# A window-attention and Fourier kernel: from row 19 on, transfers issued in the program's order

## Chip, cores and metric

The kernel runs on one core of a Trainium2 chip. The metric is the device time of one execution in microseconds, the median over runs. Everything is float32.

## What is computed

The input x is 32 images of 56 x 56 positions with 128 channels. Two layers are applied one after the other, each on a group-normalised copy of x (groups of 4 channels) and each added back to x.

```python
# layer 0: shifted 7x7-window attention, 4 heads of 32 channels, with position bias and shift mask
x = x + attention(_gn(x), rpb_table, w_qkv, w_proj, b_proj)

# layer 1
def _forward_fourier(x, w0, w1):          # x is (B, I, M, N) here
    x_fty = dct(x, norm='ortho', axis=-1)
    out_y = einsum('bixy,ioy->boxy', x_fty[..., :32], w0)
    xy = idct(out_y padded to N, norm='ortho', axis=-1)
    ...                                    # the same along the other axis with w1: xx
    return xx + xy

def _feedforward(x, W1, b1, W2, b2):       # 128 -> 512 -> 128
    return relu(x @ W1 + b1) @ W2 + b2

x = x + _feedforward(_forward_fourier(_gn(x), w0, w1), W1, b1, W2, b2)
```

## The kernel before

An image is cut into 8 rows of windows (7 lines of 56 positions each). The program is one software pipeline over *cycles*. In cycle n, row n of all images in sequence (row n mod 8 of image n div 8) gets its q, k and v, its scores and its maximum; row n-1 its exponentials; row n-2 its transpose; row n-3 its product with v, its projection and the residual sum (`attn_project`); row n-4 its sums and squares for the second normalisation. The second layer of an image starts 11 cycles after the first row of the image (`CONV_BEGIN`) and takes 16 cycles, so that two images are in it at a time; c counts its cycles. The DCT along the width is done at c = 0, along the height at c = 1 and 2, the mixing of modes at c = 3, 4 and 5, the way back at c = 5, 6, 7, 10 and 12, and the feed-forward product in seven groups of tokens at c = 8, 9, 10, 12, 13, 14 and 15. In this text *row k* stands for a cycle whose number is k modulo 8, so that c = 0 falls into rows 3, c = 1 into rows 4, c = 5 into rows 0.

Up to cycle 18 a head of its own (`first_rows`, `next_rows`) fills the pipeline. The loop from cycle `HEAD_END` = 19 on is the steady state: `halves_first`, `eighths`, `quarters`, `behind_max` and `halves_last` write down one cycle's work. When no rows are left for projection, the loop takes a branch of its own that ends each cycle with `load_first`, `last_out` and `load_back`: the drain.

The order of the instructions on PE, ACT, DVE and POOL is the order in which the program writes them (`manual_schedule`). SP, which issues nearly all transfers, is in program order only until cycle 10; then `in_order.close()` leaves its order to a scheduler, which moves transfers past each other by its own estimate of when each can run. Whatever the order, SP is one queue: an issue that waits for a semaphore holds all that stand behind it. Each transfer also carries one of eight completion semaphores in turn, and waits for the transfer eight places before it.

The transfers of the steady state are:

- `xin`, a quarter of the next image: `load_quarter` (L160) issues four transfers of 112 KB, with runs of 128 bytes, into a single buffer; `turn_quarter` transposes it on DVE (L424 to L429) into the window layout `xw`. Which quarter is turned in which row is a table, `next_steps`: in row 0 the first (0, 0) early in the row and the second (0, 1), called *late*, behind the maximum; in row 4 the third, in row 5 the fourth. A quarter that is turned early is loaded by `next_begin` at the end of the row before; a late one by `next_quarter` in its own row.
- `xr`, tokens of x for the residual sum of the row that is projected next cycle: `load_tokens` (L137), called by `next_tokens`; POOL adds the projection's bias (L143). The buffer's last reader is `sum_squares` on DVE (L752).
- `scr<-x`, the first layer's result (L722), stored to DRAM behind each projection.
- `htok`, the same result read back as columns for the DCT along the height (`load_columns`, L859, 2 x 392 KB): the first half in row 3, the second in row 4 once PE has used the first (L825), for one buffer.
- `zscr<-z` and `zT<-zscr`: mixed modes stored (L882) and read back (`load_modes`, L893, by `load_back`) for the way back on PE (`modes_back`, L911), with two buffers.
- `res`, the tokens to which the feed-forward result is added (`ff_in`, L944 and L949), two buffers; POOL adds a bias (`ff_bias`, L961), DVE adds the product (L1008, L1018), and `ff_out` stores to the output (L1024 to L1039, `out_dram<-res`).

In `ff_in` the load of `res` is written ahead of the matmuls of the same group; a scheduler may issue it earlier, as soon as the buffer is free.

Of the kernel before, what the change touches and what calls it, by code (L numbers as in the profile page):

```python
# [50 lines left out]
def swin_fourier_kernel(  # L51
# [33 lines left out]
    ET = mybir.EngineType  # L85
# [15 lines left out]
    def conv_bank():  # L101
        return conv_banks[next(conv_turns) % 4]
# [47 lines left out]
    def load_quarter(b, k, u):  # L150

        if b > 1:
            t = work.tile([P, HW, KB], F32, tag="xin", name="xin", bufs=1)
        else:
            t = y_of[k][:, : S * KB].rearrange("p (w c) -> p w c", w=S)
            t = t[:, u * HW : (u + 1) * HW]
        rows = slice(k * (S - KB), k * (S - KB) + KB)
        for cb in range(C // KB):
            cs = slice(cb * KB, (cb + 1) * KB)
            nc.sync.dma_start(t[cs], x[b, rows, u * HW : (u + 1) * HW, cs])  # L160
        return t
# [34 lines left out]
    xins = {}  # L196
# [741 lines left out]
    def ff_in(im, g):  # L938
        t0, n = sum(FF_GROUPS[:g]), FF_GROUPS[g]
        k, last = n // P, n % P  # L940
        xff = im.xf.rearrange("p r w -> p (r w)")
        scr_tok = im.scr.rearrange("h w c -> (h w) c")
        res = work.tile([P, 4, C], F32, tag="res", name="res")
        nc.sync.dma_start(  # L944
            res[:, :k], scr_tok[t0 : t0 + k * P].rearrange("(n p) c -> p n c", p=P)
        )
        if last:
            for hs in HALVES:
                nc.sync.dma_start(res[hs, k, :JP], scr_tok[t0 + k * P : t0 + n, hs])  # L949
        im.res = res  # L950
        im.hid = []
        for f in range(NF):
            ph = conv_bank()
            halved(ph[:, :n], wff1[:, f * P : (f + 1) * P], xff[:, t0 : t0 + n])
            hf = work.tile([P, HB], F32, tag="hid", name="hid", bufs=NF)
            nc.scalar.activation(hf[:, :n], ph[:, :n], AF.Relu, bias=b1sb[:, f : f + 1])  # L956
            im.hid.append(hf)
# [123 lines left out]
    def next_tokens(cycle):  # L1081
        im, i = row(cycle - 2)
        if im:
            load_tokens(im, i)
# [6 lines left out]
    def halves_first(cycle):  # L1091
        begins = [im for im, c in fourier(cycle) if c == 0]
        last, j = row(cycle - 4)
        if cycle % NWR == NWR - 1:
            norm_step(cycle)
        tokens_bias(cycle)
        im, i = row(cycle)
        behind_short = im and i == NWR - 1
        if behind_short:
            attn_q(im, i)  # L1100
            attn_exp(cycle - 1)
        if (cycle - 1) % NWR not in EARLY:
            divide(cycle)
        if last:
            attn_sums(last, j)
        next_quarter(cycle)
        if im:
            if not behind_short:
                attn_q(im, i)
            attn_k(im, i)  # L1110
            if i == NWR - 2:
                wrap_rows(cycle)
        late = squares_late(cycle)
        if last and not late:
            attn_squares(last, j)
            sum_squares(last, j)
        if not late:
            next_tokens(cycle)
        if cycle % NWR == 0:
            norm_step(cycle)  # L1120
        for im, c in fourier(cycle):
            if c in FF_AT:
                ff_in(im, FF_AT.index(c))
        for im in begins:
            if cycle > HEAD_END:
                start_stats(im)
# [102 lines left out]
    def next_steps(cycle):  # L1229
        b, i = divmod(cycle, NWR)  # L1230
        steps = {
            0: ((0, 0), (0, 1), ()),
            1: (None, None, (0, 1, 2, 3)),
            4: ((1, 0), None, ()),
            5: ((1, 1), None, (4, 5)),
            6: (None, None, (6, 7)),
        }
        if b == 0:
            steps[0] = (None, None, ())
            steps[1] = ((0, 0), None, ())  # L1240
            steps[2] = ((0, 1), None, ())
            steps[3] = (None, None, (0, 1, 2, 3))
        if b == 1:
            steps[0] = ((0, 0), None, ())
            steps[1] = ((0, 1), None, ())
            steps[2] = (None, None, (0, 1, 2, 3))
        none = (None, None, ())
        return (b + 1, *(steps.get(i, none) if b + 1 < NB else none))

    def next_quarter(cycle):  # L1250
        b, quarter, late, _ = next_steps(cycle)
        if quarter:
            turn_quarter(images[b], *quarter)
        if late and (b, *late) not in xins:
            xins[(b, *late)] = load_quarter(b, *late)

    def wrap_rows(cycle):
        b = next_steps(cycle)[0]
# [63 lines left out]
    HEAD_END = CONV_BEGIN + FF_AT[0]  # L1322
# [79 lines left out]
    def next_rows(cycle):  # L1402
        c = cycle - CONV_BEGIN
        first = images[0]
        im, i = row(cycle)
        im3, i3 = row(cycle - 3)
        last, j = row(cycle - 4)
        attn_q(im, i)
        attn_k(im, i)
        if i == NWR - 2:  # L1410
            wrap_rows(cycle)
        attn_exp(cycle - 1)
        scale_head(first, c, False)
        next_quarter(cycle)
        attn_values(im3, i3, cycle - 3, i in VALUES_BY_ACT)
        tokens_bias(cycle)
        if c == 0:
            for h in range(2):
                transform(first, True, h)
        if c in (1, 2):  # L1420
            transform(first, False, c - 1)
            if c == 1:
                load_columns(first, 1)
        attn_scores(im, i, cycle)
        attn_max(cycle)
        for h in range(2 if c == 0 else 0):
            for r in range(2):
                turn_modes(first, True, h, r)
        for r in range(2):
            columns_turn(cycle, r)  # L1430
        turn(cycle)
        for width, g in back_groups(c):
            modes_back(first, width, g)
            fetch_back(first, width, g)
        if c == 3:
            half_columns(cycle)
        if c:
            attn_squares(last, j)
            attn_sums(last, j)
        divide(cycle)  # L1440
        if c:
            sum_squares(last, j)
            if j < NWR - 1:
                add_sums(last, j)
        next_tokens(cycle)
        next_groups(cycle)
        if i == NWR - 1:
            for _ in range(2):
                norm_step(cycle)
        attn_v(im, i, cycle)  # L1450
        if i == NWR - 1:
            norm_step(cycle)
        if i == 0:
            norm_step(cycle)
        if c == 0:
            start_stats(first)
            next(first.stats)
            next(first.stats)
            load_first(cycle)
        if c != 3:  # L1460
            half_columns(cycle)
        half_columns(cycle, True)
        scale_head(first, c, True)
        load_back(cycle + 1)
        next_begin(cycle)
        attn_project(im3, i3)
        if cycle == HEAD_END - 1:
            attn_exp(cycle)
# [35 lines left out]
    in_order.close()  # L1504
    for cycle in range(CONV_BEGIN, HEAD_END):
        next_rows(cycle)
    for cycle in range(HEAD_END, NB * NWR + CONV_BEGIN + FF_AT[-1] - NWR + 1):
        halves_first(cycle)
        if not row(cycle - 3)[0]:
            eighths(cycle)  # L1510
            for r in range(2):
                columns_turn(cycle, r)
            behind_max(cycle)
            quarters(cycle)
            last_fetch(cycle)
            half_columns(cycle)
            half_columns(cycle, True)
            scale_first(cycle, 0)
            scale_first(cycle, 1)
            load_first(cycle)  # L1520
            last_out(cycle)
            load_back(cycle + 1)
            continue
        if not has_ff(cycle):
            half_columns(cycle)
        eighths(cycle)
        early = any(c == 10 for _, c in fourier(cycle))
        if early:
            columns_turn(cycle, 0)
        quarters(cycle)  # L1530
        if row(cycle)[0]:
            attn_max(cycle)
        if not early:
            columns_turn(cycle, 0)
        columns_turn(cycle, 1)
        last_fetch(cycle)
        if squares_late(cycle):
            sum_squares(*row(cycle - 4))
            next_tokens(cycle)
        behind_max(cycle)  # L1540
        load_first(cycle)
        halves_last(cycle)
# [62 lines left out]
```

## Time and profile before

| what | value |
|---|---|
| time, median of 3 runs | 3221.83 us (3219.25 to 3224.47) |
| the profiled execution | 3222.57 us, span 3220.8 us |
| busy in the span | PE 3162.6, weight loads 2369.0, DVE 2508.5, ACT 2189.3, POOL 2280.0 us |
| PE busy in 0 to 200 us | 158.0 us |
| transfers of the SP queue | 437 MB, 57% of the 16 engines' time |
| packets under 512 bytes | 513,296 of 1,160,384 |
| largest waits of SP | 626.6 us for DVE at L1032; 125.5 us for DVE at L137; 89.0 us for DVE at L160 |
| POOL's wait for `res` (L961) | 77.8 us in 12 waits, 10.7 at the longest |

A busy engine in this table is the union of its instructions' times. The span is that of the program's instructions, and the time around it is 1.8 us. An image takes eight rows, about 97 us of the steady state. The lines of the trace are those of the listing above; `SPq` names an issue by SP, which counts as idle time of SP's engine.

### The profile page before, as it was taken

What the parts mean: (1) busy time and instruction counts of PE and PEld (TensorE: products, weight loads), DVE (VectorE), ACT (ScalarE), POOL (GpSimd) and SP (SyncE); (2) the same over time, 40 slices, a digit from 0 to 9 for tenths busy, and PEclk for the clock granted to TensorE, in tenths of its full rate; (3) what the DMA queues carried; (4) which work ended last, traced back from release to release, by engine and by line L of the source; (5) the groups of instructions that cost most, each with busy time, mean ns of one, the idle gap of its engine ahead of it and who ended that gap; (6) DMA issues with size and microseconds to landing.
All of it is one profiled execution on the core that took longest, in us unless ns stands there. A gap on an engine that the chain in (4) does not pass through costs nothing.

```text
span 3220.8 us, 152669 instructions
## 1 busy us (share of the span) xinstructions
PE 3162.6 (98%) x65968; PEld 2369.0 (74%) x65968; DVE 2508.5 (78%) x4753; ACT 2189.3 (68%) x4018; POOL 2280.0 (71%) x2552
## 2 busy tenths in 40 slices
PE   7899999999999999999999999999999999999999
PEld 5667777777777777777777777777777777777776
DVE  7668888888888788888888888887888888887751
ACT  5566676676777666777766776666777666776664
POOL 5547777777777777777777777777777777777741
PEclk9999999999999999999999999999999999999999
DMA  6555665665666666556656566655556655565453
GB/s 131 111 128 132 146 141 140 141 147 141 144 142 144 138 143 148 141 141 144 140 141 148 140 141 144 140 145 145 138 140 149 139 143 141 142 144 139 123 139 102
DMA packets 1160384, 448.29 MB, mean 139 GB/s; under 512 B 513296, under 2 KB 1129857, under 8 KB 1159709
## 3 DMA queue, kind: packets, MB, share of 16 engines
q1 hardware_dynamic: 1157715, 437.49, 57.0%
q8 instruction: 517, 8.47, 1.2%
q14 instruction: 158, 1.29, 0.1%
q10 hardware_dynamic: 1642, 0.94, 0.1%
q0 software_dynamic: 352, 0.09, 0.0%
HBM read 276.77 MB, written 161.48 MB: 136 GB/s over the span
## 4 chain that ended last, share of the span: by engine, by line
PE 94%; DVE 2%; issue 1%; DMA 1%; POOL 1%; ACT 1%; SPq 0%; DVEq 0%; POOLq 0%; ACTq 0%
PE pc L129 41%; PE pa L129 10%; PE pa L545 8%; PE pc L872 7%; PE pa L567 6%; PE pa L706 6%; PE pa L661 5%; PE pc L911 5%; PE pc L825 3%; PE pc L632 1%; DMA xin<-in_x_dram 1%; PE pc L998 0%; ACT k L532 0%; PE pa L772 0%; PE pc L400 0%
## 5 line engine op out<-in xcount | busy, mean ns | idle before, releaser
L616 POOL TENSOR_TENSOR blocks<-a,rs 32x272 f32<-32x272 f32 (+3 forms) x1416 | 1202.3, 856 | 379.1 <-DVE rs L599 257.1
L129 PE MATMUL pc<-xf,wff 128*64 128x512 f32 (+2 forms) x3584 | 714.3, 539 | 0.0
L129 PE MATMUL pc<-wff,hid 128*64 128x128 f32 x12288 | 712.8, 273 | 1.3 <-issue 0.6
L129 PEld LDWEIGHTS pc<-wff,hid 128*64 128x64 f32 x12288 | 680.2, 137 | 8.2 <-issue 2.9
L586 POOL TENSOR_TENSOR a<-a,mx 128x784 f32<-128x784 f32 x249 | 374.8, 1505 | 303.6 <-DVE mx L585 289.5
L129 PEld LDWEIGHTS pc<-xf,wff 128*64 128x64 f32 x3584 | 264.9, 136 | 368.9 <-issue 293.7
L956 ACT ACTIVATE hid<-pc,b1sb 128x512 f32<-128x512 f32 (+2 forms) x896 | 500.2, 642 | 42.0 <-PE pc L129 41.9
L129 PE MATMUL pa<-xw,wn 128*64 128x392 f32 x2048 | 392.5, 498 | 8.2 <-ACT wn L498 8.1
L575 DVE TENSOR_TENSOR a<-pa,bm 128x392 f32<-128x392 f32 x498 | 257.7, 559 | 170.4 <-PE pa L567 157.8
L552 ACT COPY v<-pa 128x512 f32<-128x512 f32 x256 | 151.6, 592 | 287.4 <-PE pa L545 278.9
L143 POOL TENSOR_TENSOR xr<-xr,bproj 128x384 f32<-128x384 f32 (+1 forms) x256 | 292.5, 1142 | 59.0 <-DMA xr<-in_x_dram 35.3
L532 ACT ACTIVATE k<-pa,bqkv,heads 128x392 f32<-128x392 f32 x512 | 318.5, 673 | 16.2 <-ACT q L519 1.4
L961 POOL TENSOR_TENSOR res<-res,b2sb 128x512 f32<-128x512 f32 (+1 forms) x224 | 251.8, 1124 | 83.4 <-DMA res<-scr 77.8
L847 ACT ACTIVATE y<-modes,rstd 128x448 f32<-128x448 f32 x256 | 276.8, 1141 | 44.8 <-DVE modes L840 31.3
L519 ACT ACTIVATE q<-pa,bqkv 128x392 f32<-128x392 f32 x256 | 149.7, 585 | 231.3 <-PE pa L129 229.2
L592 ACT ACTIVATE a<-a 128x784 f32<-128x784 f32 x249 | 213.2, 856 | 128.0 <-POOL a L586 127.9
L644 DVE STREAM_TRANSPOSE eT<-blocks 128x1024 f32<-128x1024 f32 x237 | 291.2, 1229 | 0.0
L545 PE MATMUL pa<-wn,xw 128*64 128x128 f32 x4096 | 285.4, 280 | 4.2 <-issue 3.1
L661 PEld LDWEIGHTS pa<-eT,v 49*32 49x32 f32 x16384 | 172.6, 105 | 150.8 <-issue 66.8
L597 DVE TENSOR_REDUCE sm<-a 128x16 f32<-128x784 f32 x249 | 238.5, 958 | 45.9 <-ACT a L592 45.3
L545 PEld LDWEIGHTS pa<-wn,xw 128*64 128x64 f32 x4096 | 222.3, 137 | 40.2 <-issue 4.8
L585 DVE TENSOR_REDUCE mx<-a 128x16 f32<-128x784 f32 x249 | 241.1, 968 | 7.6
(136 smaller groups left out, 5017.3 us busy)
## 6 DMA issues: line engine op xcount, KB each, us to landing
zscr<-z SPq DMA_DIRECT2D x512, 112.0 KB
xin<-in_x_dram SPq DMA_DIRECT2D x480, 112.0 KB
htok<-scr SPq DMA_DIRECT2D x128, 392.0 KB
zT<-zscr SPq DMA_DIRECT2D x192, 256.0 KB
res<-scr SPq DMA_DIRECT2D x160, 256.0 KB
out_dram<-res SPq DMA_DIRECT2D x160, 256.0 KB
scr<-x SPq DMA_DIRECT2D x256, 112.0 KB
xr<-in_x_dram SPq DMA_DIRECT2D x256, 84.0 KB
```

The source lines that it names most:

```text
L129: nc.tensor.matmul(dst[ps], lhsT=lhsT[:, ps], rhs=rhs, start=start, stop=stop)
L143: nc.gpsimd.tensor_tensor(piece, piece, bproj.unsqueeze(1).to_broadcast([P, n, C]), ALU.add)
L532: nc.scalar.activation(k_sb[:, u], pk[:, :RT].rearrange("p (w j) -> p w j", j=WT), AF.Identity, bias=im.bias[:, 3 + u : 4 + u], scale=head ...
L545: nc.tensor.matmul(pv[HALVES[w % 2], w // 2 * C : (w // 2 + 1) * C], lhsT=im.half[i // NP][:, t0 : t0 + JP], rhs=im.w[:, 2 * C : 3 * C], s ...
L575: nc.vector.tensor_tensor(a[:, 2 * hp : 2 * hp + 2, :, 0:WT].rearrange("p u w j -> p w u j"), ps[hp][:, :RT].rearrange("p (w u j) -> p w u ...
L586: nc.gpsimd.tensor_tensor(a3, a3, mx.unsqueeze(2).to_broadcast([P, 2 * NWR, WT]), ALU.subtract)
L616: nc.gpsimd.tensor_tensor(dst[to, k, :, :n], a3[src, :, kb * KB : kb * KB + n], rs[src].unsqueeze(2).to_broadcast([src.stop - src.start, 2 ...
L644: nc.vector.transpose(eT.rearrange("p t (k j) -> p k t j", k=2), blocks[r % 2])
L661: nc.tensor.matmul(po4[u][h * HD : (h + 1) * HD, pr], lhsT=v[ks, pr, h * HD : (h + 1) * HD], rhs=eT[ks, h * NP + pr, :WT], start=True, sto ...
L847: nc.scalar.mul(y[:, r], t.rearrange("p (n k) -> p n k", k=NM), im.rstd)
L956: nc.scalar.activation(hf[:, :n], ph[:, :n], AF.Relu, bias=b1sb[:, f : f + 1])
L961: nc.gpsimd.tensor_tensor(im.res[:, :k], im.res[:, :k], b2sb.unsqueeze(1).to_broadcast([P, k, C]), ALU.add,)
```

## The change

From cycle 19 on SP too is in program order. To give this order a sense, the loads of quarters get a place of their own, `load_quarters`, behind the turn of the quarter and the squares, and they are issued there both for the late quarter of this row and for the early quarter of the next row. The residual tokens are moved behind `ff_in`, so that `res` is issued ahead of them. `next_quarter` keeps its load of late quarters for the head alone; `next_begin` finds its quarter loaded and only begins an image.

```diff
--- before.py
+++ after.py
@@ -1114,13 +1114,14 @@
         if last and not late:
             attn_squares(last, j)
             sum_squares(last, j)
-        if not late:
-            next_tokens(cycle)
+        load_quarters(cycle)
         if cycle % NWR == 0:
             norm_step(cycle)
         for im, c in fourier(cycle):
             if c in FF_AT:
                 ff_in(im, FF_AT.index(c))
+        if not late:
+            next_tokens(cycle)
         for im in begins:
             if cycle > HEAD_END:
                 start_stats(im)
@@ -1251,8 +1252,15 @@
         b, quarter, late, _ = next_steps(cycle)
         if quarter:
             turn_quarter(images[b], *quarter)
-        if late and (b, *late) not in xins:
+        if late and cycle < HEAD_END and (b, *late) not in xins:
             xins[(b, *late)] = load_quarter(b, *late)
+
+    def load_quarters(cycle):
+        b, _, late, _ = next_steps(cycle)
+        nb, quarter, _, _ = next_steps(cycle + 1)
+        for key in (late and (b, *late), quarter and (nb, *quarter)):
+            if key and key not in xins:
+                xins[key] = load_quarter(*key)
 
     def wrap_rows(cycle):
         b = next_steps(cycle)[0]
@@ -1504,6 +1512,7 @@
     in_order.close()
     for cycle in range(CONV_BEGIN, HEAD_END):
         next_rows(cycle)
+    ctx.enter_context(tc.manual_schedule(engines={ET.SP}))
     for cycle in range(HEAD_END, NB * NWR + CONV_BEGIN + FF_AT[-1] - NWR + 1):
         halves_first(cycle)
         if not row(cycle - 3)[0]:
```

The numbers of transfers and of all other instructions are as before, and so is the order of PE, ACT, DVE and POOL.

## The prediction

> **What bounds the kernel now.** First the page, then the busy times of three stretches, then the waits, then single rows on the queue and on PE.
>
> ```profile
> span 3220.8 us, 152669 instructions
> ...
> PE 94%; DVE 2%; issue 1%; DMA 1%; POOL 1%; ACT 1%; SPq 0%; DVEq 0%; POOLq 0%; ACTq 0%
> ```
>
> ```profile
> 200.00:3100.00 2900.00, 2888.23 (x60348) 2158.84 (x60342) 2336.45 (x4376) 2019.20 (x3698) 2161.25 (x2410) 1.00 0.59 141
> 3100.00:3221.00 121.00, 116.38 (x1748) 81.85 (x1746) 30.42 (x71) 55.69 (x92) 19.25 (x21) 1.00 0.41 114
> ```
>
> The columns are the stretch, its length, busy PE, weight loads, DVE, ACT and POOL, the granted clock, DMA share and GB/s. The edit acts from row 19 on (about 200 us). From there to 3100 us PE is idle for 2900 - 2888.2 = 11.8 us in all; that is most of what an earlier transfer can win there. The last 121 us, where attention is over and only the Fourier and feed-forward work of the last images is left, is PE too.
>
> ```profile
> DVE xw L424 <- DMA xin<-in_x_dram: 65.7, 48, 3.6
> ...
> SPq L1032 <- DVE res L1008: 626.6, 149, 9.2
> ```
>
> The figures are the wait in total, times, longest. DVE does wait for quarters (`xin`). Taken apart by place in the image: the 28 waits in rows with cycle mod 8 = 0 (31.2 us) are for the second quarter of a half, whose load needs the buffer that the same row has just turned; the change leaves that as it is. The rest, in rows 5, is what the change reaches: 28 waits of 42.5 us, ten of them put down to another transfer of the same queue. The second line is the price side: SP, which issues every transfer, stands 626.6 us before output stores that wait for DVE, and all that is behind such a store in its order stands too.
>
> **The change, part by part.** The built order of PE, DVE, ACT and POOL is the same instruction by instruction, and the same 3,246 transfers are issued. Only SP's order changes, so each term is a transfer that lands earlier or later than its reader wants it. Where I give a landing, it is from the trace's semaphore updates: from the end of an issue to the last update of that transfer.
>
> *Quarters a row ahead.* In row 4 the load of the next quarter now stands directly behind the previous store, four issues together. Before, they were split:
>
> ```profile
> 1584.23 0.32 SPq L160 DMA_DIRECT2D xin<-in_x_dram  x1
> 1584.65 0.99 SPq L137 DMA_DIRECT2D xr<-in_x_dram  x2
> 1585.68 0.39 SPq L160 DMA_DIRECT2D xin<-in_x_dram  x1
> 1586.17 1.02 SPq L859 DMA_DIRECT2D htok<-scr  x2
> 1587.23 2.72 SPq L160 DMA_DIRECT2D xin<-in_x_dram  x2
> ```
>
> ```profile
> 1595.55 1.12 DVE L424 STREAM_TRANSPOSE xw<-xin 128x512 f32<-128x512 f32 x1 [1.13 <-DMA xin<-in_x_dram]
> ```
>
> The last two quarters went behind the column tokens (`htok`), landed at 1595.04 and 1595.36, and DVE waited 1.13 us. In the 28 bursts of four that the trace has elsewhere, the last lands 5.7 us after the first issue: here 1590, five us before DVE wants it. What PE gains is less than DVE's 42.5 us: the interval between projections that ends in row 5 is 13.51 us in the mean over 28 images and 13.41 at the least, so 28 x 0.10 = 2.7 us. Bounds 0 and 2.7; I take 2.7, since the wait goes altogether. In rows 1 and 2 quarters no longer crowd the queue; the interval that ends in row 2 has 28 x 0.24 = 6.7 us over its least one, where PE stands a microsecond inside a run of matmuls that wait for nothing shown. The same traffic moves into rows 3, 4 and 7, so bounds +6.7 and -6.7 us; I take half the gain, 3.3.
>
> *Column tokens later.* The cover of that gain is the slack of `htok`. Its second load, issued at 1586.68, landed at 1594.79, and PE reads it here:
>
> ```profile
> 1597.34 1.11 PE L825 MATMUL pc<-htok,dct_h 56*32 56x448 f32 x16
> ```
>
> That is 2.55 us of slack; over 31 images 1.10 to 3.89, median 2.72. In the new order four quarters, the residual tile (`res`, 256 KB) and two token loads stand ahead of it, and a mode load (`zT`, 256 KB) directly behind. The DMA engines are full from 1585 to 1594 (shares of 0.87, 1.04 and 1.14 in stretches of 3 us), so work ahead counts in full: landings in a burst of quarters are 1.0 us apart, those of 392 KB token loads 2.1 to 2.6, which makes 256 KB 1.5 us. Least shift: 1.5 (the residual tile alone, as the other two quarters were in flight beside the tokens already). Most: 1.5 + 2 x 1.0 + 0.5 for the share of the mode load = 4.0. Summing what exceeds the slack image by image: 0.7 us in all at 1.5, 11.3 at 2.8, 37.5 at 4.0. I take 2.8, midway: +11.3. The first `htok` load (issued in row 3, now behind four quarters instead of none) has a median slack of 4.94, least 2.03: 0 to 3.7 us, I take 1.
>
> *Residual tiles and tokens.* `res` was fetched up to a row ahead; now it stands in its own row behind quarters. In row 4 it would land near 1591.2, 1.0 us after POOL wants it (L961 at 1590.23), in row 0 some 2 us after. Behind that instruction on POOL stands the next division (L616, six instructions, 5.35 us); it starts at 1592.60, when DVE's reciprocal is there, and the bias then ends at 1592.5. So nothing, with POOL's idle time as the cover; were it gone, 1 us a row in two rows of 29 images is 58 us at the most. Residual tokens (`xr`) are issued two to four issues later (1 to 2 us) and have 5 to 11 us of slack in rows 3 to 5: nothing.
>
> *The drain.* Here the scheduler's freedom was worth something. In the loop's last branch `load_back` stands behind `last_out`, so in program order each mode load goes behind an output store that waits for DVE, where it had gone ahead or well before:
>
> ```profile
> 3161.12 0.40 SPq L1032 DMA_DIRECT2D out_dram<-res  x1
> 3163.45 0.38 SPq L944 DMA_DIRECT2D res<-scr  x1
> 3164.38 0.91 SPq L893 DMA_DIRECT2D zT<-zscr  x2
> 3167.46 0.38 SPq L1032 DMA_DIRECT2D out_dram<-res  x1
> 3167.89 1.13 SPq L1039 DMA_DIRECT2D out_dram<-res  x2
> ```
>
> ```profile
> 3162.59 1.38 PE L911 MATMUL pc<-idcth,zT 64*64 64x112 f32 x48
> 3168.66 1.82 PE L911 MATMUL pc<-idctw,zT 64*64 64x112 f32 x64
> ```
>
> Take the second: stores end at 3169.02, the mode load's issue at 3169.4, its landing (median 2.92 us over 192 loads) at 3172.36; PE wants it at 3168.66, so 3.7 us of PE. The same for the six places where PE reads modes behind a store or the column writes: 3143.86 wants what comes at 3146.87 (3.0), 3153.23 at 3154.16 (0.9), 3162.59 at 3164.86 (2.3), 3168.66 (3.7), 3189.62 at 3190.57 (1.0), 3197.63 at 3198.5 (0.9): 11.8 us. PE has nothing else in its order, so they add. The very last residual tile goes from 3211.74 to behind the stores that end at 3215.56; landing 1.9 and bias 0.73 us later make 3218.6, against the end of the last matmul at 3216.9: 1.7. Together 13.5; at the least 9, if the eight column writes issue without the 2 us break they had and landings are at the tenth percentile (2.54).
>
> A page of the Trainium skill, "DMA: Bandwidth & Descriptors", says in its section on the anatomy of one DMA that semaphore waits happen on the issuing sequencer, ahead of dispatch; the 626.6 us row is that, and it is what speaks against a fixed order here. The same section gives 2.0 us plus bytes by 436 GB/s, as its measure for the GpSimd path; that would put a mode load at 2.6 us, against 3.3 in this trace with its issue, and take some 4 us off the drain and all of the stall on column tokens, a sum near 3226 us as an estimate. The trace's rows are what I use.
>
> *Sum*: -2.7 - 3.3 + 11.3 + 1 + 13.5 = +19.8 us. The profiled execution took 3222.57 us, 1.8 of them around its span; it stands 0.7 above the median of 3221.83, so the forecast is 3241 us.
>
> **Rivals.** *Much slower*: the shift of the column tokens is its upper bound, 4.0 us, and PE stands in every row 5. For it: no gap in DMA traffic there. Against: the quarters overlapped the tokens before. 37.5 + 3.7 + 13.5 = 55: 3276 us. It decides from a shift of about 3.3 us. *No change*: the tokens keep their slack (shift 1.5, 0.7 us), crowding is really relieved (-6.7 and -2.7) and the drain costs its least, 9: 3222 us. That program order is near the old order would end here as well, but the built order has the four quarters, then `res`, then tokens in every such row. *Faster*: DVE, freed of 42.5 us, is the hidden pace of PE, and all 11.8 us of idle PE in 200 to 3100 us go; for it, the chain passes through two `xin` loads in rows 4 (15.8 us of it). With the drain at its least cost, 9, that is 3219 us; it decides once rows 200 to 3100 us give back more than the drain takes, 9 to 13.5. Against: PE is 99.6% busy in that stretch, so the price of the drain exceeds the prize.
>
> **How the numbers follow.** Forecast 0.66, much slower 0.16, no change 0.11, faster 0.07. What this kernel's measurement can tell from no change is about 0.2%, 6.4 us. Low end: the drain at its least, 9, tokens 0.7, gains of 6: 3226. High end: drain 13.5, tokens at a shift of about 3.7 (30): 3265. Slower by over 0.2% takes the forecast and the first rival: 0.82; within, 0.11; faster, 0.07.
>
> **What would show it.** Right: PE's idle time in the last 121 us grows by about 10 us, before L911 matmuls that `zT` ends; DVE's wait on `xin` falls to near 31 us, all in rows 0; PE waits for `htok` at L825 in rows 5, some 0.4 us an image; POOL's wait on `res` grows without cost. Wrong: a drain as long as before; row 5 unchanged or shorter; or new waits of POOL that reach PE through the division.

## The result, and the profile after

| | before | after |
|---|---|---|
| median | 3221.38 us (4 runs, 3219.25 to 3224.47) | 3244.16 us (4 runs, 3241.90 to 3245.18) |
| ratio | | 1.0057 [1.0045, 1.0070] |
| span of the profiled execution | 3220.8 us | 3243.4 us |
| last projection to the end | 111.9 us | 130.0 us |

By these medians the edit costs 23 us; the forecast was 3241 (3221.83 and 19.8 make 3241.6). The medians divide to 1.0071, while the recorded ratio of 1.0057 stands for 18 us. The same two kernels differ by 17.5 us in `c_after` (one execution, beside the 3219.10 of its chip) and by 17.8 in `f1_after_again`, both below, so the cost is known as 18 to 23 us. Where the time lies is seen first in the busy times of three stretches of the changed kernel (stretch, length, busy PE, weight loads, DVE, ACT, POOL, granted clock, DMA share, GB/s):

```profile
0.00:200.00 200.00, 156.39 (x3668) 124.62 (x3668) 137.18 (x300) 111.17 (x224) 97.34 (x120) 0.93 0.54 116
200.00:3100.00 2900.00, 2890.42 (x60432) 2162.61 (x60434) 2336.74 (x4380) 2020.16 (x3696) 2163.82 (x2408) 1.00 0.60 142
3100.00:3244.00 144.00, 124.69 (x1872) 88.93 (x1866) 33.70 (x76) 58.98 (x99) 20.52 (x24) 0.95 0.37 101
```

PE is idle for 9.6 us between 200 and 3100 us, 2.2 us less than before. The end is what grew: 19.3 us without PE where there were 4.6, and a granted clock of 0.95 where it was 1.00. The waits of the whole execution (in total, times, longest):

```profile
POOL res L961 <- DMA res<-scr: 187.8, 71, 12.5
...
DVE xw L424 <- DMA xin<-in_x_dram: 36.8, 27, 6.1
...
PE pc L911 <- DMA zT<-zscr: 12.4, 8, 3.7
```

DVE's wait for quarters fell from 65.7 to 36.8 us, POOL's wait for residual tiles rose from 77.8 to 187.8. The third line is new; before, PE did not wait for modes. Six of its eight waits, 11.1 us, stand in the drain. On PE's timeline of the drain it is this (the idle time ahead of a row, and what ended it, stand in brackets):

```profile
3150.64 0.61 PE L911 MATMUL pc<-idctw,zT 64*64 64x112 f32 x16 [2.26 <-DMA zT<-zscr]
3151.18 3.59 PE L872 MATMUL pc<-w0sb,y 128*64 128x128 f32 x32
...
3174.46 1.86 PE L911 MATMUL pc<-idcth,zT 64*64 64x112 f32 x48 [2.44 <-DMA zT<-zscr]
3176.25 3.11 PE L129 MATMUL pc<-wff,hid 128*64 128x128 f32 x32
...
3185.53 3.27 PE L911 MATMUL pc<-idctw,zT 64*64 64x112 f32 x64 [3.72 <-DMA zT<-zscr]
```

The last row waits 3.72 us, and the forecast for it was 3.7. But it then takes 3.27 us where the same 64 matmuls took 1.82 before, and the L872 group behind the first wait takes 3.59 us for the 1.97 of before:

```profile
3144.40 1.97 PE L872 MATMUL pc<-w0sb,y 128*64 128x128 f32 x32
```

Busy times of two short stretches of the same execution, with the clock as the eighth figure:

```profile
3151.30:3154.70 3.40, 3.40 (x34) 3.40 (x36) 0.69 (x2) 0.58 (x1) 1.27 (x1) 0.50 0.02 9
...
3185.50:3188.90 3.40, 3.38 (x66) 3.12 (x68) 1.17 (x3) 0.00 (x0) 0.73 (x1) 0.50 0.14 41
```

PE runs at half its clock for 3.41 us behind each of the three longest waits. The transfer that PE waits for at 3185.53 is issued here, behind the stores, as in the forecast:

```profile
3180.59 0.38 SPq L1032 DMA_DIRECT2D out_dram<-res  x1
3181.09 1.13 SPq L1039 DMA_DIRECT2D out_dram<-res  x2
3182.31 1.09 SPq L893 DMA_DIRECT2D zT<-zscr  x2
```

One thing in the pair of profiles fits no part of the forecast. Projections counted from 0 to 255, number 15 (cycle 18, ahead of the edit's reach) starts at 201.2 us before and at 208.7 after: 7.5 us of the 22.6 by which the two spans differ. The rest is -3.0 us from there to the last projection and 18.1 us in the drain.

### The profile page after: what moved, and what is told of

Its sections match the earlier page's. It is cut to its first block, busy times and chain, and to the rows that moved or that the text cites. A ratio compares the mean times of both kernels' runs of the same rounds, so it can differ in the third digit from the quotient of the medians.

```text
span 3243.4 us, 152408 instructions
## 1 busy us (share of the span) xinstructions
PE 3171.5 (98%) x65968; PEld 2376.2 (73%) x65968; DVE 2507.6 (77%) x4753; ACT 2190.3 (68%) x4018; POOL 2281.7 (70%) x2552
## 4 chain that ended last, share of the span: by engine, by line
PE 94%; DVE 2%; DMA 2%; issue 1%; SPq 1%; ACT 1%; POOL 0%; DVEq 0%; POOLq 0%; ACTq 0%
PE pc L129 41%; PE pa L129 10%; PE pa L545 8%; PE pc L872 7%; PE pa L567 6%; PE pa L706 6%; PE pc L911 6%; PE pa L661 5%; PE pc L825 3%; PE pc L632 1%; DMA zT<-zscr 1%; PE pc L998 0%; DMA xin<-in_x_dram 0%; PE pa L772 0%; DVE mx L585 0%
## 5 line engine op out<-in xcount | busy, mean ns | idle before, releaser
L129 PE MATMUL pc<-xf,wff 128*64 128x512 f32 (+2 forms) x3584 | 714.4, 539 | 0.1
L129 PE MATMUL pc<-wff,hid 128*64 128x128 f32 x12288 | 713.4, 273 | 0.3 <-ACT xf L934 0.3
L129 PEld LDWEIGHTS pc<-wff,hid 128*64 128x64 f32 x12288 | 681.7, 137 | 5.9 <-issue 2.0
L129 PEld LDWEIGHTS pc<-xf,wff 128*64 128x64 f32 x3584 | 264.8, 136 | 369.1 <-issue 290.1
L129 PE MATMUL pa<-xw,wn 128*64 128x392 f32 x2048 | 393.5, 499 | 10.8 <-ACT wn L498 7.9
L961 POOL TENSOR_TENSOR res<-res,b2sb 128x512 f32<-128x512 f32 (+1 forms) x224 | 251.7, 1124 | 196.9 <-DMA res<-scr 187.8
```

What stands on the lines that cost most here:

```text
L129: nc.tensor.matmul(dst[ps], lhsT=lhsT[:, ps], rhs=rhs, start=start, stop=stop)
L961: nc.gpsimd.tensor_tensor(im.res[:, :k], im.res[:, :k], b2sb.unsqueeze(1).to_broadcast([P, k, C]), ALU.add,)
```

## The experiments

In the expectations "the projection of row 15" is projection number 15 and "row 16" is number 16, in cycle 19. Elsewhere rows are counted modulo 8, as above. The drain is the time from the start of projection 255 to the end of the span.

### Head: both kernels once more

> The kernel before, unchanged, for its head. The profile of the changed kernel reached the projection of row 15 (cycle 18) 7.5 us later than the profile of before, at code that is nearly the same. Theory C1 (the head varies from one execution to the next): this profile's head differs from the first profile of before by 2 us or more, in step with the stretches at clock 0.5, and the total stays within 3219 to 3225 us. Theory C2 (the edit does it): the same row within 1 us of the first profile.

> The changed kernel, unchanged, for its head and its drain. C1: the head differs from the first profile of after by 2 us or more. C2: it again stands about 7.5 us behind before at the projection of row 15. Theory A (the drain's mode loads behind the output stores): from the last projection to the end again 129 to 131 us, PE waiting 12 to 13 us for zT at L911, and clock 0.5 behind the longest of these waits.

Measured, one execution each: before 3224.83 us, after 3236.58 us, with projection 15 at 207.5 and 204.4 us. So the order of the two is reversed: the head varies by itself. The time at clock 0.5 in the head goes with it. Over all fourteen profiles of the study, from the trace's record of the clock:

```
profile        half clock 30-215 us   projection 15 starts at
e1_modes_ahead        10.2                 198.5
e3, e4                13.7                 202.3, 202.4
before, e5, e6        17.1                 201.2, 204.1, 202.6
f2, f4                17.1                 203.6, 202.8
e2_drain_alone        20.5                 202.7
c_after, f1, f3       27.3                 204.4, 206.6, 205.1
after                 30.7                 208.7
c_before              34.1                 207.5
```

The 7.5 us are not the edit's. The drain of the second profile of after is 127.3 us, below the 129 to 131 that theory A had, that of before 111.4.

### The drain put right, and the drain alone

```diff
             load_first(cycle)
-            last_out(cycle)
             load_back(cycle + 1)
+            last_out(cycle)
             continue
```

> The changed kernel with one edit undone in effect: in the drain the mode loads of the next cycle stand ahead of the output stores again, all else in program order. Theory A (the drain pays some 18 us, 12.4 in waits for zT, 4.2 in half clock behind them, 1.5 at the last tile): 3228 to 3231 us, PE's waits for zT at L911 near 0, the drain 113 to 116 us, no 0.5 clock in it. Theory B (the steady rows' order of quarters, residual tiles and column tokens costs the time, the drain little): 3238 us or more. Theory A2 (only the waits themselves were lost; the half clock is not their doing): 3232 us with 0.5 clock still in the drain.

Measured: 3225.49 us beside 3219.10, ratio 1.0018 [1.0009, 1.0027]; drain 116.6 us. The two mode loads now stand ahead of the store:

```profile
3159.33 0.92 SPq L893 DMA_DIRECT2D zT<-zscr  x2
3163.11 0.38 SPq L1032 DMA_DIRECT2D out_dram<-res  x1
```

```profile
3164.24 1.76 PE L911 MATMUL pc<-idctw,zT 64*64 64x112 f32 x64
```

No wait is left where 3.72 us stood. Two others are: 1.61 us at a group whose load stands behind eight column writes (issued to 3136.98), and 1.16 us at one whose load still stands behind the store of the cycle before (issued at 3190.47). With the later last tile (2.0 us, below) they make 4.8 of the 4.9 us that this drain is above before's. No half clock appears in it ahead of its last microseconds. Theory A holds in the drain, though its figure of 113 to 116 us left this remainder too small; the time lies below its 3228 to 3231.

The other direction, the kernel before with a fixed order in the drain only:

```diff
     for cycle in range(HEAD_END, ...):
+        if cycle == NB * NWR + 3:
+            ctx.enter_context(tc.manual_schedule(engines={ET.SP}))
         halves_first(cycle)
```

> The kernel before with SP in program order in the drain alone (from cycle 259); rows before it as before. Theory A: 3237 to 3240 us, the whole drain of after (129 to 131 us from the last projection to the end) on the rows of before. Theory B: 3222 to 3228 us. If the head's 7.5 us come from the edit (C2) and the rows give back 3, A gives 3239; if they are chance (C1), the same 3239, since the head here is that of before.

Measured: 3236.54 us, ratio 1.0055 [1.0042, 1.0067], drain 126.9 us, just below what theory A had for both. The changed kernel has 1.0057, and 1.0054 when repeated (`f1_after_again`): the drain alone is its whole loss, within the intervals.

### The steady rows by themselves

```diff
-    ctx.enter_context(tc.manual_schedule(engines={ET.SP}))
+    fixed = ctx.enter_context(ExitStack())
+    fixed.enter_context(tc.manual_schedule(engines={ET.SP}))
     for cycle in range(HEAD_END, ...):
+        if cycle == NB * NWR + 3:
+            fixed.close()
         halves_first(cycle)
```

> The changed kernel up to the last projection, and SP given back to the scheduler in the drain (from cycle 259). Theory A (the whole loss is the drain's order): the drain is 111 to 113 us again, from the projection of row 16 to the last one 2887 to 2890 us as in the two profiles of after (2889.3, 2887.7), and the time is 0 to 3 us below the kernel before of the same call (ratio 0.9990 to 1.0002). Theory C2 (the edit lengthens the head by 4 to 7 us): ratio 1.001 to 1.002. Theory B (steady rows cost time): above 1.002.

Measured: 3225.06 us beside 3226.46, ratio 1.0000 [0.9990, 1.0009]; drain 112.6 us. This ran on another chip, where before itself takes longer; its 2894.5 us from projection 16 to the last are not to be set beside the 2887.7 to 2892.3 of the four profiles of before and after so far. The ratios, each taken on one chip, can be compared: the steady rows neither win nor lose by the edit, within 3 us.

That does not say that its parts are nothing:

```diff
 # on top of e3_drain_free
+        if not late:
+            next_tokens(cycle)
-        load_quarters(cycle)
...
-        if not late:
-            next_tokens(cycle)
...
-        if late and cycle < HEAD_END and (b, *late) not in xins:
+        if late and (b, *late) not in xins:
```

> SP in program order from row 19 to the last projection, but quarters and residual tokens at the places in the program that they had before; the drain left to the scheduler. Beside e3_drain_free it tells the fixed order from the quarters a row ahead. Theory Q (the 3 us that the rows gave back are the quarters'): DVE waits for xin over 60 us again, from row 16 to the last projection 2890 to 2893 us, the 28 intervals that end in row 0 sum to 431 us (after 429.0 to 429.5), the time 0 to 3 us above e3_drain_free. Theory P (they come from the fixed order): 2887 to 2889 us, 429 us, the time of e3_drain_free.

Measured: 3431.72 us, ratio 1.0658 [1.0631, 1.0684]. Both theories missed it by 200 us. The timeline of all engines in a row 0:

```profile
1634.64 3.13 SPq L160 DMA_DIRECT2D xin<-in_x_dram  x4
...
1640.73 1.10 DVE L424 STREAM_TRANSPOSE xw<-xin 128x512 f32<-128x512 f32 x1 [3.83 <-DMA xin<-in_x_dram]
...
1642.82 0.14 DVE L502 COPY bqkv<-pa 128x1 f32<-128x1 f32 x1
...
1643.01 0.49 PE L567 MATMUL pa<-k,q 64*49 64x98 f32 x8 [3.36 <-DVE bqkv L502]
```

The quarter's load ends its issue at 1637.8, DVE stands for it until 1640.73, the bias copy that PE's scores need is behind that transpose in DVE's order, and PE waits 3.36 us. DVE's wait for `xin` is 273.9 us in this run, PE's for that copy 88.2 us in 28 waits, for L691 (also on DVE) 48.6, and 129.7 us between 215 us and the drain run at half clock, some 65 us of work lost: together 202 of the 205. Beside e3_drain_free, on the same chip, the 28 intervals that end in rows 0 grow by 135 us and those in rows 5 by 52. What differs is the lead, from the end of an early quarter's last issue to its transpose, median in rows 0, 4 and 5: 19.0, 18.8 and 4.9 us in before, 3.0, 2.5 and 2.4 here, 10.6, 10.3 and 8.2 in e3_drain_free. The scheduler had been issuing quarters early all along; the fixed order takes that away and `load_quarters` gives it back.

> The changed kernel without the fixed order: quarters and residual tokens at their new places in the program, SP left to the scheduler all along. With before (free order, old places), e6_order_alone (fixed, old: +205 us) and e3_drain_free (fixed, new: 0) it is the fourth corner. Theory S (the scheduler puts the quarters early by itself, so their place in the program matters only under a fixed order): ratio 0.999 to 1.001, drain 111 to 113 us. Theory Q (the quarters a row ahead gain by themselves): 0.997 to 0.999, 3 to 9 us below before.

The edit is the deletion of the line that fixes the order. Measured: 3221.09 us beside 3220.72, ratio 1.0001 [0.9992, 1.0010], drain 111.8 us. Theory S holds: with a free order the place in the program makes no difference to the time.

```diff
 # on top of e3_drain_free
+        if not late:
+            next_tokens(cycle)
         load_quarters(cycle)
...
-        if not late:
-            next_tokens(cycle)
```

> e3_drain_free with the residual tokens at their old place, ahead of the quarters and the residual tile, instead of behind them. By the forecast they have 5 to 11 us of slack: the same time within 3 us (ratio 0.999 to 1.001), POOL's wait for xr (34 us in e3_drain_free) shorter. Rival: the tokens ahead push the column tokens later still, PE's bursts at L825 in rows 5 over 33 us (before 29.5, e3_drain_free 33.1) and the time up by as much, or the quarters, and DVE's wait for xin rises above 48 us.

Measured: 3244.51 us, ratio 1.0074 [1.0061, 1.0086]; the drain is 112.3 us, so 24 us are lost in the rows. The forecast's "nothing" for this part was wrong, and of the rival's two ways the first is a small share: the bursts at L825 sum to 35.1 us. The queue of this run in row 4, then of e3_drain_free:

```profile
1592.54 0.92 SPq L722 DMA_DIRECT2D scr<-x  x2
1595.20 0.78 SPq L137 DMA_DIRECT2D xr<-in_x_dram  x2
1596.03 2.15 SPq L160 DMA_DIRECT2D xin<-in_x_dram  x4
1598.22 2.01 SPq L944 DMA_DIRECT2D res<-scr  x1
```

```profile
1583.97 0.90 SPq L722 DMA_DIRECT2D scr<-x  x2
1586.25 2.08 SPq L160 DMA_DIRECT2D xin<-in_x_dram  x4
1588.38 0.55 SPq L944 DMA_DIRECT2D res<-scr  x1
```

From the start of the store to the end of the issue of `res` it is 7.7 us here and 5.0 there: the tokens wait 1.7 us for their buffer and take 0.8 to issue, the quarters stand behind them (alone they had waited 1.4), and the issue of `res` itself takes 2.0 us instead of 0.6. The waits of this run:

```profile
POOL res L961 <- DMA res<-scr: 312.8, 112, 11.3
...
DVE res L1008 <- POOL res L961: 129.2, 93, 4.4
```

POOL waited 171.9 us and DVE 53.3 in e3_drain_free. `f1_after_again` (below) has the same steady rows but for the tokens' place and ran on the same chip. Beside it the intervals between projections grow by 14 us in rows 5, 6 in rows 2 and 6 in rows 3, over 28 images. By the time from one group of matmuls to the next, 5.1 us of this stand at L825, 10.2 at the first feed-forward product (`pc<-xf,wff`) of rows 2 and 5, whose banks DVE frees, and 6.4 at L772 in rows 3, which waits for DVE's sums here (4.9 us, 0.2 in f1_after_again). DVE's wait for POOL's `res` is 36.6 us in rows 2, where there was none, and 46.6 in rows 5 for 2.7. So most of the 24 us lie where DVE is late, and 5 at the column tokens; no run tests the two ways apart.

### Column tokens later still

```diff
+        for im, c in fourier(cycle):
+            if c == 1 and cycle > HEAD_END and row(cycle)[0]:
+                tok = im.scr.rearrange("h w c -> (h w) c")
+                nc.sync.dma_start(
+                    again.rearrange("(n p) c -> p n c", p=P),
+                    tok[: 4 * P].rearrange("(n p) c -> p n c", p=P),
+                )
```

> The changed kernel with one more transfer of 256 KB (rows of the residual again, to a place in DRAM that nobody reads) ahead of the second column-token load of each image. In the two profiles of after that load lands 0.70 and 1.02 us (median) before PE reads it. Theory T (what exceeds the slack is PE's, image by image; the shift of the forecast was too large, its price per us right): a shift of 1.5 us costs 17 to 25 us, from row 16 to the last projection 2905 to 2914 us, the time 3254 to 3262 us, PE waiting for htok at L825 0.5 to 0.9 us an image. Theory T2 (PE's wait for the tokens is absorbed by another wait in the same row): under 6 us, 3236 to 3250 us. Theory T3 (a transfer ahead overlaps and does not delay the tokens): the slack keeps its median and the time stays at 3236 to 3245 us.

Measured: 3253.82 us, ratio 1.0087 [1.0073, 1.0101]. Read from the trace, for 28 images, in rows 5: when the second column tokens have landed after the projection that ends row 4 (PE reads them 6.37 us after it), their slack, and the sum of the times from the first matmul that reads them to the next group:

```
profile              landed (median)   slack (median)   bursts at L825, sum
before                    3.74 us          2.64 us           29.5 us
after                     5.85             0.53              30.9
e3_drain_free             6.07             0.30              33.1
e4_tokens_later           6.66            -0.26              40.5
```

The extra 256 KB moved the tokens by 0.6 us, not 1.5. From the start of the two loads' issue to their landing it is 7.87 us in e3_drain_free and 7.88 here (medians); the issue starts 0.56 us later. So the transfer ahead delayed the tokens by its place in SP's queue, not by its bytes. PE's price is 7.4 us above e3_drain_free on the same chip. Against the slack of before the landing is now 2.9 us later and costs 11 us; the forecast's sum has 11.3 for 2.8 us and 13.1 for 2.9. So theory T in its price, with a time just under its 3254 to 3262, and near T3 in how little a transfer ahead delays.

### The half clock

```diff
     px = [conv_bank(), conv_bank()]
+    for _ in range(FILL.get((im.b, width, g), 0)):
+        nc.tensor.matmul(attn_banks[0][: P // 2], lhsT=wff1[:, : P // 2],
+                         rhs=wff1[:, :HB], start=True, stop=True)
```

> The changed kernel with 4, 4 and 7 matmuls (0.45 us each, 1.8, 1.8 and 3.15 us) into a bank that nobody reads, ahead of the L911 matmuls behind the three longest waits of the drain (2.2, 2.2 to 2.4 and 3.7 us). Theory D (the half clock follows PE's idle time): the three waits shrink to 0.3 to 0.8 us, no stretch at clock 0.5 in the drain ahead of its last microseconds, from the last projection to the end 124.5 to 126 us (after: 130.0 and 127.3 with three and two such stretches); the time 2 to 4 us below after. Theory D2 (the half clock comes from something else, such as the amount of transfers, or is chance): two or three such stretches again, 127 to 130 us, the time that of after.

Measured: 3249.93 us, ratio 1.0070 [1.0057, 1.0082]; no stretch at clock 0.5 in the drain ahead of its last microseconds, but a drain of 131.1 us. (`FILL` names the three groups behind the longest waits, with 4, 4 and 7 matmuls.) The fill was mis-sized: the records show two for each matmul, and eight of them take 3.60 us: 0.9 us a matmul, not 0.45. So 13.4 us of fill stood in 8 us of waits. It was repeated with half as much, beside the changed kernel:

> The changed kernel, unchanged, timed beside the next run on the same chip. Theory A: ratio to before 1.0045 to 1.0070 again; two or three stretches at clock 0.5 in the drain ahead of its last microseconds, from the last projection to the end 127 to 130 us.

> The changed kernel with 2, 2 and 4 matmuls (0.9 us each as measured in e5_fill_waits: 1.8, 1.8 and 3.6 us) into a bank that nobody reads, ahead of the same three waits, so that they fill the waits and do not outlast them. Theory D (half clock follows PE's idle time): no 0.5 stretch in the drain ahead of its end, 125 to 126.5 us from the last projection to the end, the time 2 to 4 us below f1_after_again. Theory D2 (it does not): the stretches stay and 127 to 130 us.

Measured: after 3238.55 us, ratio 1.0054 [1.0041, 1.0066]; filled 3235.84, ratio 1.0048 [1.0035, 1.0062]; the drains are 126.4 and 126.0 us. PE in the filled run:

```profile
3173.34 3.60 PE L910 MATMUL pa<-wff 128*64 128x512 f32 x8
3177.18 1.89 PE L920 MATMUL pc<-idctw,zT 64*64 64x112 f32 x64 [0.25 <-DMA zT<-zscr]
```

The same group as at 3185.53 above (its line is L920 here) takes 1.89 us again. The accounts of the drains, against 111.65 for the mean of the two before (waits of PE over 0.3 us; the end is what lies behind the last matmul, 3.9 us before):

```
profile          drain over 111.65   waits   fill   end   left over   half-clock stretches
after                 18.4            12.0    -     2.0      4.4       3 of 3.41 us
c_after               15.6            10.8    -     2.0      2.9       2 of 3.41
e2_drain_alone        15.2            10.4    -     2.0      2.8       2 of 3.41
e4_tokens_later       15.6            10.4    -     1.7      3.5       2 of 3.41
f1_after_again        14.8            10.5    -     2.0      2.3       1 of 6.83
e5_fill_waits         19.5             4.8  13.4    2.0     -0.8       none
f2_fill_short         14.3             5.0   7.4    1.7      0.3       none
```

The times don't tell f2_fill_short from f1_after_again: the intervals overlap. The traces do: what is left over is there with the stretches and gone without them. Theory D holds.

## Why the prediction was right, and where not

**The drain** was the right mechanism at the right places. Its waits were forecast at 11.8 us and are 10.4 to 12.0; the last residual tile at 1.7 and is 2.0. The step that fell short is "together 13.5": the sum of waits has no price for the work behind a wait. Half clock adds 2.3 to 4.4 us. A page of the Trainium skill, "TensorE: Matmul & The Clock Gate", says in its Part 1, on the clock gate, that PE falls to half rate after about one idle window of 3.4 us, on a window that runs freely. The stretches of 3.41 and 6.83 us agree with such a window. But waits of 2.08 to 2.44 us were followed by half clock in five cases (two in the first profile of after, one each in c_after, e2_drain_alone and e4_tokens_later), and waits of 2.02, 2.20 and 2.22 us in three cases (e4_tokens_later, f1_after_again and c_after) were not. So here a wait shorter than a whole window could do it; what decides between these cases was not settled.

**Column tokens** ("I take 2.8, midway: +11.3") is the term that was most off. The shift was 2.1 us, for which the forecast's own sum gives 3.5, and the rise of the bursts at L825 is 0.2 to 4 us, by which profiles are set beside each other. The price per microsecond was near, as e4_tokens_later shows; wrong was "work ahead counts in full". Counted from the projection that ends row 4, the two loads' issue starts 4.85 us ahead in before and 1.73 in after, where seven transfers are issued ahead of it instead of four; but from that start to the landing it is 8.55 us in before and 7.86 in after. The work ahead made the issue late and the transfer no longer. "Row 5 unchanged or shorter" was one of the forecast's signs of being wrong, and rows 5 did stay as they were (below). The slack of 1.10 to 3.89 us and the three sums hold for the 28 images of the steady rows, not for 31. The first load's +1 shows as 0.3 us (28 intervals that end in row 4, over the profiles named next).

**Quarters earlier and crowding** (-2.7, -3.3): DVE's wait fell nearly as forecast, and most of what is left stands in rows 0 (30.2 us). Over seven profiles (before, c_before, e2 against after, c_after, e1, f1) the 28 intervals that end in row 0 shrink by 1.8 us, rows 1 by 0.9, rows 2 by 1.1, rows 7 grow by 0.5, rows 5 stay: -3.0 in all with the tokens' price in it. So gains of 3.8 us show, but only 1.1 of them in a row that the forecast named; in rows 5 a gain could stand hidden behind the tokens' price. The timed ratio of e3_drain_free, 1.0000, can't tell them from nothing.

**Residual tiles and tokens at nothing** holds for the edit as it is: POOL's waits grew by 110 us and cost nothing that can be measured. But it is the narrowest step. The forecast saw POOL's idle time as cover; in f4_tokens_ahead `res` is issued 2.7 us later behind its store, POOL and DVE wait, and with the later column tokens 24 us are gone.

**What the forecast did not see** is that the three parts of the edit belong together. Timed ratios to before, the drain left free in all:

| order of SP | quarters at the old place | quarters a row ahead, tokens ahead | quarters a row ahead, tokens behind |
|---|---|---|---|
| free | 1 (before) | not tried | 1.0001 |
| fixed | 1.0658 | 1.0074 | 1.0000 |

The fixed order costs 205 us, the quarters give back some 180 of them, the tokens behind them the other 24. The forecast set only the orders of before and after beside each other, and so took the quarters for a gain of a few microseconds; their lead is what the fixed order lives on.

That the total came out so near is in part luck. In the first pair of profiles the rows gave -3.0 us where the forecast had +6.3, the drain took 18.1 where it had 13.5, and the head, of which it said nothing, happened to take 7.5: 22.6 in all. The error in the rows is that of the tokens' price, about 9 us, and the other two made up for it.

Of the rivals, "no change" had the tokens nearly right (0.7 us at a shift of 1.5) and the drain wrong; "much slower" fell with the shift; "faster" fell with e3_drain_free.

No version here beats before. The best of the changed kernel, with the drain given back to the scheduler, is its equal.

## To carry to other kernels

A fixed order of a queue is right or wrong place by place: look at the lead of each transfer over its reader, and at branches such as a drain, where loads that feed the bound engine may stand behind stores that wait. Where an edit has several parts, price each without the others: a sum near nothing may be +205, -180 and -24. To the price of a wait on PE belongs the work that may run at half clock behind it.

## What was not expected of the hardware

A PE wait of little over 2 us can be followed by 3.41 us at half clock (behind 2.26 us, L872: 3.59 us for 1.97), and with the waits filled by matmuls into an unused bank the clock stayed at 1.00 in both runs that tried it, up to the drain's last microseconds. A transfer of 256 KB ahead in SP's queue made the next one land 0.6 us later and its issue start 0.56 us later, so of its bytes nothing is seen. The head's length goes with its time at half clock, 198.5 us at 10.2 us and 207.5 to 208.7 at 31 to 34, for nearly the same code; which of the two is the cause was not tested. And matmuls of 128x64 weights by 512 columns, all into the same half of a bank's partitions, took 0.9 us each (8 records in 3.60 us); the kernel's own, which alternate between the halves, take half of that (L129 `pc<-xf,wff`, 16 records in 3.60 us).
